# Long score products of heads 2 and 3 with 128 keys at once, between products with 64

## The chip, the cores and the metric

The kernel runs on one core of a Trainium2 chip. The metric is the device time of one execution in microseconds (us); a comparison is made on medians of several executions. The engines that matter here are TensorE (PE in the profile, with PEld for its weight loads), VectorE (DVE), ScalarE (ACT) and GpSimd (POOL). SyncE (SP) issues transfers.

## The reference

Thirty-two images of 256 channels and 32 x 32 = 1024 positions are normalized in 32 groups of channels, go through a causal attention of 8 heads with 32 channels each, and are added to the result. All is float32. Cut to the core:

```python
n = group_norm(x)                                   # 32 groups of 8 channels
q, k, v = q_w @ n + q_b, kv_w @ n + kv_b            # 256 channels each, 8 heads of 32
scores = einsum('bhqd,bhkd->bhqk', q, k) / sqrt(32)
attn = softmax(where(mask == 0, -10000, scores))    # mask: keys before the query alone
attn = where(mask == 0, 0, attn)
x = x + einsum('bhqk,bhkd->bhqd', attn, v)
```

## The kernel before

The 8 heads are two groups g of four, since four heads of 32 channels fill the 128 partitions: head j of a group lies in partitions 32j to 32j + 31 of the group's q and k. The 1024 queries are two halves of 512, and the keys are blocks of 128. Scores are made transposed, keys on partitions and queries along the free axis, so that their exponential can go straight into the product with v.

The work is cut into pieces (`piece`): a full piece is one key block against 512 queries (or, on the diagonal, one block against 384 queries and a second block against 128: two entries in `blocks`), a half piece one key block against 256 queries. A visit takes one full and one half piece of the four heads. Each group has 6 visits, an image 12, and the 32 images 384; in this document a visit and what is done beside it is called a round. In one third of the rounds the full piece has two blocks.

The loop over i runs through all rounds of all images. On TensorE a round has three stages: the scores of visit i (`scores`, matmuls in line 285), then a share of the projections of the next image (`product`, line 158: tiles pp and ppv), and then the values, the products of the exponentials of the visit before with v (`values`, line 373: tile acc). The order on TensorE, ScalarE, VectorE and GpSimd is the order in which the program names the work; no scheduler moves it.

Inside `scores`, three PSUM tiles of two banks each are taken: `pairs[0]` for the long products (the full piece) of heads 0 and 1, `pairs[1]` for those of heads 2 and 3, `pairs[2]` for the short products (the half piece) of all four, where head j and head j + 2 share a bank. A product contracts over the 32 channels of one head, so it occupies 32 rows of the array; its columns are the keys. `scores_of` makes it in pieces of `WIDE` = 64 keys, so a block of 128 keys takes two matmuls, with 64 columns of the array each. In the profile such a matmul has the shape 32*64 (rows * columns); the matmuls of projections and values are 128*32.

The order within the stage: short products of heads 2 and 3 (`first`), long products of heads 0 and 1 and then of 2 and 3 (for a piece of two blocks, the first block of all heads, then the second), and last the short products of heads 0 and 1. Before these last, TensorE waits on the semaphore `bank_free`, which the first short products raise, since the two share banks. The very last visit with a diagonal has an order of its own (the `else` branch). Then ScalarE takes three exponentials: of `pairs[0]`, `pairs[1]` (line 348) and `pairs[2]` (line 346), with 128 x 1024 elements each. GpSimd masks the diagonals (line 301), and VectorE adds up the exponentials for the softmax's denominators (line 381).

Of the kernel before, what the change touches and what calls it, by code (L numbers as in the profile page):

```python
# [17 lines left out]
P = 128  # L18
# [10 lines left out]
WIDE = 64  # L29
# [3 lines left out]
def tile_norm_attention_residual(  # L33
# [65 lines left out]
    def unshifted():  # L99
        live = {}  # L100
# [175 lines left out]
                blocks = [(k, slice(0, HALF), slice(0, HALF))]  # L276
            return g, hf, k, part, tuple(blocks)

        def scores_of(pc, pair, j, n=0):

            b, (g, hf, k, part, blocks) = pc
            rows = slice(HD * j, HD * (j + 1))
            kb, cols, of = blocks[n]
            return [
                nc.tensor.matmul(  # L285
                    pair[c : c + WIDE, cols], lhsT=live["k", b, g][rows, kb * P + c : kb * P + c + WIDE],
                    rhs=live["q", b, g][rows, hf * HALF + of.start : hf * HALF + of.stop],
                    start=True, stop=True, skip_group_check=True,
                )
                for c in range(0, P, WIDE)  # L290
            ]

        def mask(pc, e, heads=slice(0, 4)):


            g, hf, k, part, blocks = pc
            if k < hf * BPH:
                return
            n = len(blocks)
            diagonal = e[:, heads, : n * P].rearrange("p j (n q) -> p j n q", q=P)  # L300
            nc.gpsimd.affine_select(  # L301
                out=diagonal, in_=diagonal, pattern=[[0, heads.stop - heads.start], [0, n], [1, P]],
                compare_op=ALU.is_gt, fill=0.0, base=0, channel_multiplier=-1,
            )
            if k == 0:
                nc.gpsimd.memset(e[0:1, heads, 0:1], 1.0)

        def scores(b, full, half):


            tag = "e0" if full[2] == 0 else "e"
            name = f"{b}_{full[0]}_{full[1]}_{full[2]}"
            e = epool.tile([P, 4, HALF], F32, tag=tag, bufs=4 if tag == "e0" else 3, name=f"{tag}_{name}")
            eh = epool.tile([P, 4, HALFBANK], F32, tag="eh", bufs=4, name=f"eh_{name}")
            pairs = [ps_s.tile([P, 2, HALF], F32, tag="sT", name=f"sT_{name}_{a}") for a in range(3)]
            short = pairs[2].rearrange("p bank (n q) -> p bank n q", n=2)
            last = b == B - 1 and full[:2] == (NG - 1, NH - 1) and half[2] == NB - 2
            short_of = lambda heads, n: [m for j in heads for m in scores_of((b, half), short[:, j % 2, n, :], j)]
            long_of = lambda heads, n: [scores_of((b, full), pairs[j // 2][:, j % 2, :], j, n) for j in heads]


            if not last:
                first = short_of((2, 3), 1)
                for n in range(len(full[4])):
                    long_of(range(4), n)
            else:

                long_of(range(4), 0)
                long_of((0, 1), 1)
                first = short_of((2, 3), 1)  # L330
                long_of((2, 3), 1)

            for ins in first:
                ins.then_inc(bank_free, 1)
                tc.no_tile_sem_insts.add(ins.ins.name)
            live["free"] = live.get("free", 0) + len(first)
            wait = nc.tensor.wait_ge(bank_free, live["free"])
            for ins in first:
                tc.declare_no_dep(wait.ins, ins.ins, reason="the semaphore orders them")
            for j in range(2):  # L340
                for lo in scores_of((b, half), short[:, j, 0, :], j):
                    for ins in first:
                        tc.declare_no_dep(lo.ins, ins.ins, reason="the semaphore orders them")
            for a in range(3):
                if a == 2:
                    exp = nc.scalar.activation(eh.rearrange("p (n bank) q -> p bank n q", n=2), short, AF.Exp)  # L346
                else:
                    nc.scalar.activation(e[:, 2 * a : 2 * a + 2, :], pairs[a], AF.Exp)  # L348

            for ins in first:  # L350
                tc.add_to_no_dep_group(f"first_{name}", ins.ins)
                tc.add_to_no_dep_group("first", ins.ins)
            tc.declare_no_dep(exp.ins, group=f"first_{name}", reason="through the last two products")
            tc.declare_fence(exp.ins, group=f"first_{name}")
            for heads in (range(2), range(2, 4)) if last else (range(4),):
                mask(full, e, slice(heads.start, heads.stop))
            mask(half, eh)
            live["e", b, full], live["e", b, half] = e, eh
# [187 lines left out]
        with tc.manual_schedule(engines={ENG.PE, ENG.Activation, ENG.DVE, ENG.Pool}):  # L546
# [36 lines left out]
            for b in range(B):  # L583
                first, last = b * N, b == B - 1
# [30 lines left out]
            for i in range(B * N + 1):  # L615
                if i < B * N:
                    scores(i // N, *visits[i % N])
                for f in at.pop(i, ()):
                    f()
                pcs = products[(i - 1) % N] if i else ()  # L620
                if i == B * N:

                    sums(3, pcs, False)
                for pc in pcs:
                    values((i - 1) // N, pc, i <= (B - 1) * N or pc not in by_pe)
                if i == B * N - 2:

                    sums(3, [None, *pcs])
                if i == B * N - 1:
                    sums(3, pcs)  # L630
                for f in after.pop(i, ()):
                    f()
# [172 lines left out]
```

## Time and profile before

| | |
|---|---|
| median of 3 runs | 1822.24 us (1820.97 to 1822.68) |
| the profiled execution's own time | 1821.87 us |
| its span, first to last instruction | 1820.1 us |
| TensorE busy | 1807.9 us, 99% of the span |
| VectorE busy | 1655.6 us, 91% |
| ScalarE busy | 1480.0 us, 81% |
| GpSimd busy | 798.9 us, 44% |
| TensorE clock granted | 0.998 |

In a line of the profile, "L285 PE MATMUL sT<-q,k 32*64 32x256 f32 x14336 | 601.3, 447 | 0.2" would read: the matmuls of line 285 on TensorE write tile sT from q and k; the array shape is 32 rows by 64 columns, the moving operand has 32 partitions and 256 elements; there are 14336 of them; together they cover 601.3 us, one lasts 447 ns in the mean, and the engine was idle for 0.2 us before them. Matmuls overlap one another, so the mean of one times their number is far more than the time covered. The end of a matmul is modelled: what is sure is when it starts. A timeline line gives start and duration in us, and the number of instructions merged into it; the bracket at its end gives the idle time before, and what ended it.

### The profile page before, as it was taken

The page shows a single profiled execution, that of the slowest core. Times are in us where ns is not written, and L with a number is a line of the kernel's source. Part 1 is how long each engine was busy: PE and PEld are TensorE (multiplying, and loading weights), DVE is VectorE, ACT ScalarE, POOL GpSimd, SP SyncE. Part 2 cuts the span into 40 slices and gives each one's busy share as a digit, 9 for nine tenths or more (in the row PEclk, how much of TensorE's full clock was granted, in tenths as well). Part 3 has the DMA queues.
Part 4 walks back from the last instruction along what each step waited for, and adds up shares of the span by engine and source line. Part 5 has one row for each costly group of instructions (what it writes and reads, how often), then busy time and mean ns, then how long its engine had stood idle before and what let it go on. Part 6 is the DMA issues. An engine that isn't in the chain of part 4 may idle for free. (4 is left out here: it accounts for less than half of the span.)

```text
span 1820.1 us, 68098 instructions
## 1 busy us (share of the span) xinstructions
PE 1807.9 (99%) x30388; PEld 837.4 (46%) x30388; DVE 1655.6 (91%) x1762; ACT 1480.0 (81%) x1860; POOL 798.9 (44%) x774
## 2 busy tenths in 40 slices
PE   9999999999999999999999999999999999999997
PEld 5444444444444444444444444444444444444443
DVE  4799999999999999999999999999999999999988
ACT  6888878888888888788887888877888878888885
POOL 1444544535435445344354353443444544435532
PEclk9999999999999999999999999999999999999999
DMA  3457676676776766767767667676667676676662
GB/s 123 71 98 137 134 150 113 133 148 125 147 127 125 143 128 137 148 121 133 142 129 147 116 135 150 124 141 136 123 137 136 134 152 115 129 152 124 124 124 73
DMA packets 77836, 235.91 MB, mean 130 GB/s; under 512 B 20320, under 2 KB 21344, under 8 KB 61664
## 3 DMA queue, kind: packets, MB, share of 16 engines
q0 software_dynamic: 15872, 97.53, 40.1%
q1 hardware_dynamic: 61664, 133.96, 26.4%
q8 instruction: 239, 3.92, 0.9%
q14 instruction: 61, 0.50, 0.1%
HBM read 66.85 MB, written 34.57 MB: 56 GB/s over the span
## 5 line engine op out<-in xcount | busy, mean ns | idle before, releaser
L348 ACT ACTIVATE e<-sT 128x1024 f32<-128x1024 f32 x768 | 745.2, 1022 | 269.3 <-PE sT L285 214.5
L381 DVE TENSOR_TENSOR e<-e,e 128x1536 f32<-128x1536 f32 x376 | 632.5, 1682 | 17.7
L381 DVE TENSOR_TENSOR e<-e,eh 128x1024 f32<-128x1024 f32 x380 | 524.2, 1394 | 112.3 <-PE acc L373 92.8
L301 POOL TENSOR_SCALAR_AFFINE_SELECT e<-e 128x512 f32<-128x512 f32 (+1 forms) x257 | 381.9, 1486 | 549.6 <-ACT e L348 546.4
L285 PE MATMUL sT<-q,k 32*64 32x256 f32 (+3 forms) x14336 | 601.3, 447 | 0.2
L158 PE MATMUL pp<-xn,wT 128*32 128x512 f32 x4096 | 492.4, 598 | 0.1
L285 PEld LDWEIGHTS sT<-q,k 32*64 32x64 f32 x14336 | 353.3, 130 | 212.9 <-ACT eh L346 64.7
L373 PE MATMUL acc<-e,v 128*32 128x512 f32 (+2 forms) x4096 | 400.8, 486 | 0.0
L346 ACT ACTIVATE eh<-sT 128x1024 f32<-128x1024 f32 x384 | 395.6, 1030 | 0.0
L397 POOL DMA_DIRECT2D e<-e x248 | 202.0, 824 | 399.5 <-DMA e<-e 305.3
L158 PE MATMUL ppv<-wT,xn 128*32 128x256 f32 x4096 | 247.5, 382 | 0.0
L373 PEld LDWEIGHTS acc<-e,v 128*32 128x32 f32 x4096 | 133.1, 110 | 223.1 <-issue 192.1
L373 PE MATMUL acc<-eh,v 128*32 128x256 f32 x3072 | 224.6, 379 | 0.0
L158 PEld LDWEIGHTS pp<-xn,wT 128*32 128x32 f32 x4096 | 107.5, 109 | 237.2 <-issue 228.9
L373 PEld LDWEIGHTS acc<-eh,v 128*32 128x32 f32 x3072 | 98.8, 110 | 164.0 <-issue 153.0
L158 PEld LDWEIGHTS ppv<-wT,xn 128*32 128x32 f32 x4096 | 120.3, 109 | 110.8 <-issue 44.7
L301 POOL TENSOR_SCALAR_AFFINE_SELECT eh<-eh 128x512 f32<-128x512 f32 x128 | 166.7, 1302 | 0.6 <-ACT eh L346 0.2
L224 ACT ACTIVATE xn<-x,shift,rstd 128x512 f32<-128x512 f32 x124 | 103.1, 831 | 0.0
L484 DVE SCALAR_TENSOR_TENSOR rb<-rb,v_bias_col,x 128x512 f32<-128x512 f32 x124 | 94.0, 758 | 4.4
L238 ACT ACTIVATE k<-pp,qk_bias 128x512 f32<-128x512 f32 x128 | 89.8, 702 | 2.3 <-PE pp L158 1.2
L238 ACT ACTIVATE q<-pp,qk_bias 128x512 f32<-128x512 f32 x128 | 89.9, 702 | 1.0 <-PE pp L158 1.0
L410 DVE STREAM_TRANSPOSE turned<-folded 128x512 f32<-128x512 f32 x124 | 87.6, 706 | 2.2
(70 smaller groups left out, 665.8 us busy)
## 6 DMA issues: line engine op xcount, KB each, us to landing
e<-e POOLq DMA_DIRECT2D x124, 512.0 KB, 6.8
x<-in_x_dram SPq DMA_DIRECT2D x64, 512.0 KB, 6.3
e<-e POOLq DMA_DIRECT2D x124, 256.0 KB, 4.6
folded<-e SPq DMA_DIRECT2D x124, 256.0 KB, 3.9
rb<-inverses SPq DMA_DIRECT2D x124, 256.0 KB, 8.0
out_dram<-rb SPq DMA_DIRECT2D x124, 256.0 KB, 4.7
inverses<-inv_turned SPq DMA_DIRECT2D x31, 32.0 KB, 1.7
out_dram<-rb_last SPq DMA_DIRECT2D x3, 256.0 KB, 2.5
```

The source lines that it names most:

```text
L158: nc.tensor.matmul(out[part], lhsT=lhsT[:, part], rhs=rhs, start=start, stop=stop, skip_group_check=True)
L224: nc.scalar.activation(xn, xt, AF.Identity, bias=live["shift", b][:, g : g + 1], scale=rstd)
L238: nc.scalar.activation(live[key][:, cols], pp, AF.Identity, bias=qk_bias[:, n, g : g + 1], scale=(SCALE, 1.0)[n],)
L285: nc.tensor.matmul(pair[c : c + WIDE, cols], lhsT=live["k", b, g][rows, kb * P + c : kb * P + c + WIDE], rhs=live["q", b, g][rows, hf * HA ...
L301: nc.gpsimd.affine_select(out=diagonal, in_=diagonal, pattern=[[0, heads.stop - heads.start], [0, n], [1, P]], compare_op=ALU.is_gt, fill= ...
L346: exp = nc.scalar.activation(eh.rearrange("p (n bank) q -> p bank n q", n=2), short, AF.Exp)
L348: nc.scalar.activation(e[:, 2 * a : 2 * a + 2, :], pairs[a], AF.Exp)
L373: nc.tensor.matmul(acc[HD * j : HD * (j + 1), of], lhsT=live["v", b][:, kb, h * HD : (h + 1) * HD], rhs=e[:, j, cols], start=first, stop=l ...
L381: nc.vector.tensor_add(total[:, :, of], total[:, :, of], e[:, :, cols])
L397: nc.gpsimd.dma_start(out=total[:rows], in_=total[rows : 2 * rows], accum_op=ALU.add)
L410: nc.vector.transpose(turned, live["folded", b][:, j, :])
L484: nc.vector.scalar_tensor_tensor(rb, rb, v_bias_col[:, g : g + 1], xt[:, g, cols], ALU.add, ALU.add)
```

## The change

`scores_of` gets a parameter for the number of keys that a matmul takes, 128 unless it is told otherwise, and `short_of` and `long_of` hand it on. In every visit but the last, all products are still told 64, except the long ones of heads 2 and 3 (of the first block, where there are two), which come between the long products of heads 0 and 1 and what follows, and are now made as one matmul of 128 keys for each head, shape 32*128. In the last visit's own order the second blocks of all heads and the first short products take 128 keys. The short products that come last stay at 64.

```diff
-        def scores_of(pc, pair, j, n=0):
+        def scores_of(pc, pair, j, n=0, wide=P):
...
-                    pair[c : c + WIDE, cols], lhsT=live["k", b, g][rows, kb * P + c : kb * P + c + WIDE],
+                    pair[c : c + wide, cols], lhsT=live["k", b, g][rows, kb * P + c : kb * P + c + wide],
...
-                for c in range(0, P, WIDE)
+                for c in range(0, P, wide)
...
-            short_of = lambda heads, n: [m for j in heads for m in scores_of((b, half), short[:, j % 2, n, :], j)]
-            long_of = lambda heads, n: [scores_of((b, full), pairs[j // 2][:, j % 2, :], j, n) for j in heads]
+            short_of = lambda heads, n, wide=P: [
+                m for j in heads for m in scores_of((b, half), short[:, j % 2, n, :], j, 0, wide)
+            ]
+            long_of = lambda heads, n, wide=P: [
+                scores_of((b, full), pairs[j // 2][:, j % 2, :], j, n, wide) for j in heads
+            ]
...
-                first = short_of((2, 3), 1)
-                for n in range(len(full[4])):
-                    long_of(range(4), n)
+                first = short_of((2, 3), 1, WIDE)
+                long_of((0, 1), 0, WIDE)
+                long_of((2, 3), 0)
+                for n in range(1, len(full[4])):
+                    long_of(range(4), n, WIDE)
             else:
-                long_of(range(4), 0)
+                long_of(range(4), 0, WIDE)
                 long_of((0, 1), 1)
                 first = short_of((2, 3), 1)
                 long_of((2, 3), 1)
...
-                for lo in scores_of((b, half), short[:, j, 0, :], j):
+                for lo in scores_of((b, half), short[:, j, 0, :], j, 0, WIDE):
```

## The prediction

> **What bounds the kernel now.** I read the page first (shares, slices, costliest groups), then the groups kept apart by shape, then the timeline of one round in the middle of the run, then that round's matmuls in very narrow windows, and last the waits. The page's shares and groups:
>
> ```profile
> PE 1807.9 (99%) x30388; PEld 837.4 (46%) x30388; DVE 1655.6 (91%) x1762; ACT 1480.0 (81%) x1860; POOL 798.9 (44%) x774
> L285 PE MATMUL sT<-q,k 32*64 32x256 f32 (+3 forms) x14336 | 601.3, 447 | 0.2
> L346 ACT ACTIVATE eh<-sT 128x1024 f32<-128x1024 f32 x384 | 395.6, 1030 | 0.0
> ```
>
> PE is busy all the time and waits before L285 for 0.2 us in all; L346 counts 384 rounds (one short exponential each). So a microsecond added to PE in every round is a microsecond of the kernel. The timeline of a round (start, duration, engine, instructions; PE and PEld lines alone):
>
> ```profile
> 904.09 0.40 PE L373 MATMUL acc<-eh,v 128*32 128x256 f32 x4
> 904.42 0.64 PEld L285 LDWEIGHTS sT<-q,k 32*64 32x64 f32 x24 [0.41 <-issue]
> 904.42 1.55 PE L285 MATMUL sT<-q,k 32*64 32x256 f32 x32
> 905.25 0.27 PEld L285 LDWEIGHTS sT<-q,k 32*64 32x64 f32 x8 [0.19 <-PE sT L285]
> 905.90 0.16 PEld L158 LDWEIGHTS pp<-xn,wT 128*32 128x32 f32 x8 [0.38 <-issue]
> ...
> 906.35 0.13 PEld L158 LDWEIGHTS pp<-xn,wT 128*32 128x32 f32 x4 [0.30 <-issue]
> 906.78 0.13 PEld L158 LDWEIGHTS pp<-xn,wT 128*32 128x32 f32 x4 [0.30 <-issue]
> 907.21 0.13 PEld L373 LDWEIGHTS acc<-e,v 128*32 128x32 f32 x4 [0.30 <-issue]
> ```
>
> The score stage runs from 904.42 to 905.90: 1.48 us. It holds 16 products in the program but 32 matmuls on PE, so every float32 product makes two passes. In the projection after it, four column tiles (128*32) stream together and a new set of four starts every 0.43 us (906.35, 906.78, 907.21): 0.43 us is one pass over 512 columns, so 0.32, 0.215 and 0.107 for 384, 256 and 128. Now the arithmetic of the stage: heads 0 and 1 (array rows 0 to 63) have a long product (512) and a short one (256), 2 x 0.43 + 2 x 0.215 = 1.29 us; heads 2 and 3 (rows 64 to 127) have the same. The stage takes 1.48, not 2.58, so the two pairs of heads stream side by side, in different rows.
>
> Narrow windows in that stage (groups of matmuls by shape, their mean ns last but one column) show what a first pass pays:
>
> ```profile
> L285 PE MATMUL sT<-q,k 32*64 32x512 f32 x4 | 0.7, 638 | 0.0
> L285 PE MATMUL sT<-q,k 32*64 32x256 f32 x4 | 0.4, 425 | 0.0
> ...
> L285 PE MATMUL sT<-q,k 32*64 32x256 f32 x4 | 0.4, 374 | 0.0
> L285 PE MATMUL sT<-q,k 32*64 32x512 f32 x8 | 0.6, 587 | 0.0
> ```
>
> The first two lines are the passes just after the change from 128*32 to 32*64, the last two later passes: 51 ns longer each. The last values matmuls start at 904.11 and stream 0.215 us, to 904.33; the first load of the scores starts at 904.42. So **a change of tile shape costs 0.09 us in which nothing streams, and then an exposed weight load of 0.05 us**. Within one shape there is no such gap: the loads at 906.35 to 907.21 are pulled ahead under the matmuls that are streaming.
>
> **What the Trainium skill says.** "TensorEngine Tiling (Array Packing)", section Key Properties: changing the tiling mode, not just the tile, drains TensorE; its list of modes has 32x64 and 32x128 as two. The 0.09 us, the same from 128*32 to 32*64 and back (the stage's last matmuls start at 905.59, stream to 905.81, next load 905.90), agrees. But there all rows of the array change hands, so this trace doesn't show that rows which nobody else wants are drained too. "TensorE: Matmul & The Clock Gate", section LDWEIGHTS, prices a load at its columns / 1.2 ns: 27, 53 and 107 ns for 32, 64 and 128 columns. The trace's exposed part is 25 ns for 32 columns (617 against 592 ns in the projection) and 51 for 64: it agrees. Same page, section "What happens when you issue a matmul": weight loads are pulled ahead of running matmuls; the trace agrees within a shape.
>
> **The change, part by part.** In each of 383 rounds the long products of heads 2 and 3 (first block) go from four of 64 keys to two of 128: with two passes, 4 fewer matmuls and 4 fewer loads on PE, the same columns streamed (2 x 0.43 per row group, both halves of the keys already streamed side by side). The fewer instructions are worth nothing: they are issued 7 ns apart under streams of 430. No wait, DMA or instruction of another engine moves; the order of the queues is otherwise the same. What is added: PE passes short 2,3 and long 0,1 in shape 32*64, then long 2,3 in 32*128, then short 0,1 in 32*64: two more changes of shape inside a stage that had none. I take it that each drains the whole array. Times from the stage's start, one block (256 rounds):
>
> - long 0,1 starts its first pass at 0.03, second at 0.53 (0.43 + 0.05 exposed load + stagger), streams to 0.955. Short 2,3 has been done since 0.50, and its rows now stand idle.
> - drain 0.095: 1.05.
> - long 2,3 alone: exposed load of 128 columns, two passes: 0.107 + 2 x 0.43 + 0.007 stagger: 2.02. Rows 0 to 63 idle.
> - drain 0.095: 2.11. Short 0,1: 0.05 + 2 x 0.215 + 0.02: 2.61; then 0.09 to the next stage: 2.70.
>
> Against 1.48 that is **+1.22 us**. Check of the same bookkeeping on before: short 0,1 starts at 0.94 (when long 0,1 is done) and adds 0.43 + 0.02 + 0.09: 1.48. So 1.22 is the later start of short 0,1 (2.11 - 0.94 = 1.17) and its exposed load (0.05).
>
> Two blocks (127 rounds, 384 then 128 columns; 1.52 us now): long 0,1 to 0.74, drain to 0.835, long 2,3 0.107 + 2 x 0.32 + 0.01 to 1.59, drain to 1.69; then the 128-column blocks of all heads, 0.05 + 2 x 0.107 to 1.95, short 0,1 to 2.42, and 0.09: 2.51. **+1.0 us**.
>
> The last round has its own order (three products there also go to 128 keys): two changes of shape between stages that are otherwise parallel, 0.2 + 0.15 and some imbalance: +0.7 us at most.
>
> The unknown terms. The exposed 128-column load: the nearest row,
>
> ```profile
> L144 PEld LDWEIGHTS busy<-ident 128*128 128x128 f32 x6 | 0.7, 192 | 0.0
> ```
>
> lasts 192 ns, and loads of 32 and 64 columns (110 and 132 ns when hidden) expose 25 and 51, that is all but 81 to 85; 192 less 84 is 108, as the skill's price has it. Low end 55 (the transposes' first matmul, 327 ns against 272 later): -20 us over 384 rounds; high end the whole load, 192: +33. If the second pass's load were not pulled ahead either, another 0.11 to 0.19 a round, +41 to +74. A gain is excluded, as the load was hidden before. The drain: 0.06 to 0.11 a change, -27 to +12 us.
>
> What gives back: nothing on PE, which has no idle time to fill (0.2 us). What might wait anew: the next score stage needs the banks that ScalarE's exponentials free. Long 2,3 is done at 2.0 and short 0,1 at 2.6 of the stage, and exponentials of 1.0 us each end at about 4.3; a copy of k or q behind them (projection done at 2.70 + 1.74 = 4.44, copy 0.7 us) ends at about 5.3. The next stage starts at 4.62 + 1.22 = 5.84 (a round is 904.42 to 909.04 now). So nothing waits; ScalarE and VectorE keep their work (1480 and 1656 us) in a longer span and don't bound. That leaves 0.5 us of cover; a copy later than that would hold the next score stage up by the difference.
>
> Sum: 256 x 1.22 + 127 x 1.0 + 0.7 = 312 + 127 + 1 = +440. The profiled execution took 1821.9 us with a span of 1820.1; the median is 1822.2. Span after 2260; time **2262 us**.
>
> **The rivals.** *No drain where rows don't conflict* (not slower): PE may run 32*128 in rows 64 to 127 while 32*64 streams in rows 0 to 63. Then long 2,3 starts when short 2,3 is done, as now, and short 0,1 when long 0,1 is done; the stage ends at 1.48. For it: the tiles of the pairs share neither rows nor banks, and weight loads overlap across rows. Against: the 0.09 us in which no load is pulled ahead whenever the shape changes, and the skill's sentence. It decides if a change costs heads 2 and 3 under 0.03 us (their stream ends at 905.78, the stage's at 905.81): 1822 us, within 3 either way.
>
> *A change costs only the rows concerned*: rows 64 to 127 take drain and load twice, rows 0 to 63 run on. Long 2,3 then ends at 0.50 + 0.095 + 0.107 + 0.87 = 1.57 and the stage at 1.66: +0.18; with two blocks, a change more, +0.3. 256 x 0.18 + 127 x 0.3 = 84: 1906 us. For it: row groups have their own order of passes. Against: as above.
>
> That the change isn't what it says is excluded: the compiled order of PE has two 128-key products where four of 64 stood, and the other queues are identical.
>
> **How the numbers follow.** Whole drain 0.84, rows alone 0.07, none 0.09. The whole drain's terms give 2262 - 47 (both low ends) to 2262 + 57 (high load, high drain and a little of the second pass's load), so 2215 to 2320; that holds nearly all of its 0.84 and so 8 in 10 by itself. About 0.2% is what a measurement of this kernel tells from no change: of the last case 0.06 fall within it and 0.03 are faster.
>
> **What would show it.** L285's matmuls fall from 14336 to 12792 (383 x 4 + 12 fewer), 1544 of them 32*128. The one-block stage lasts 2.7 us, the two-block one 2.5. Inside it the loads of 32*128 start some 0.09 us after long 0,1 has streamed out; the first 32*128 pass is about 107 ns longer than the second. ScalarE's wait for L285 grows. If the loads of 32*128 instead start at about 0.5 us, while long 0,1 streams, the drain isn't there and I am wrong; if only the spacing of the stage's parts is off, a term of the sum is.

## The result and the profile after

The changed kernel takes 2250.62 us (four runs, 2250.35 to 2250.9) against 1821.61 us of the kernel before beside it: a ratio of 1.2356, 95% interval 1.2334 to 1.2377. Its profiled execution has a span of 2248.9 us, 428.8 more than the 1820.1 before.

The page of the changed kernel, shares and one cause of waiting:

```profile
PE 2236.9 (99%) x28844; PEld 796.7 (35%) x28844; DVE 1601.4 (71%) x1762; ACT 1540.7 (69%) x1860; POOL 771.6 (34%) x774
L354 ACT ACTIVATE e<-sT 128x1024 f32<-128x1024 f32 x768 | 770.6, 1023 | 435.2 <-PE sT L285 360.5
L285 PE MATMUL sT<-q,k 32*64 32x256 f32 x12792 | 1033.9, 448 | 0.0
```

PE has 1544 fewer matmuls and yet 429 us more of busy time; L285 covers 1033.9 us where it covered 601.3. (Its line in the page stands for all shapes, of which it names one.) The other engines have the same instructions in a longer span, and ScalarE's wait for the scores has grown from 214.5 to 360.5 us. The groups kept apart by shape show the new products; the first line is of the kernel before, the others of the changed one:

```profile
L285 PE MATMUL sT<-q,k 32*64 32x512 f32 x4096 | 382.0, 600 | 0.0
L285 PE MATMUL sT<-q,k 32*128 32x512 f32 x1024 | 288.6, 640 | 0.0
L285 PE MATMUL sT<-q,k 32*64 32x512 f32 x2048 | 278.3, 613 | 0.0
L285 PE MATMUL sT<-q,k 32*128 32x384 f32 x508 | 116.1, 533 | 0.0
L285 PE MATMUL sT<-q,k 32*64 32x384 f32 x1032 | 112.0, 507 | 0.0
```

Of the 512-query matmuls, 4096 covered 382.0 us before; now 3072 cover 288.6 + 278.3 = 566.9. One lasts 613 or 640 ns in the mean where it lasted 600, so the matmuls have hardly become slower: fewer of them run side by side.

The timeline of one score stage with one block, weight loads alone (start, duration, engine, instructions, idle time before):

```profile
1104.36 0.13 PEld L379 LDWEIGHTS acc<-eh,v 128*32 128x32 f32 x4 [0.30 <-issue]
1104.90 0.23 PEld L285 LDWEIGHTS sT<-q,k 32*64 32x64 f32 x16 [0.41 <-issue]
1105.94 0.30 PEld L285 LDWEIGHTS sT<-q,k 32*128 32x128 f32 x4 [0.81 <-ACT xn L224]
1107.00 0.21 PEld L285 LDWEIGHTS sT<-q,k 32*64 32x64 f32 x8 [0.76 <-issue]
1107.59 0.16 PEld L158 LDWEIGHTS pp<-xn,wT 128*32 128x32 f32 x8 [0.39 <-issue]
```

Before, 24 loads of the stage came in one group and the last 8 while matmuls were streaming. Now there are three groups, one for each stretch of one shape. The last second-pass matmul of long 0,1 starts at 1105.425 and streams 512 columns, 0.43 us, to 1105.85; the loads of the 32*128 products start at 1105.94, 0.09 us later. The short products of heads 2 and 3, in the rows that these loads want, had streamed out at about 1105.40: those rows stood idle for half a microsecond. The same 0.09 us stands before 1107.00, where the products of heads 0 and 1 in turn wait for the 32*128 ones. (The release that the bracket at 1105.94 names, a ScalarE instruction, is only the last semaphore update before: in all 384 rounds, at both changes of shape, the load stands the same 0.09 us behind the end of the stream, to within 4 ns.)

Two narrow windows in the same stage show the first 32*128 pass, and the second:

```profile
L285 PE MATMUL sT<-q,k 32*128 32x512 f32 x2 | 0.7, 692 | 0.0
...
L285 PE MATMUL sT<-q,k 32*128 32x512 f32 x2 | 0.6, 587 | 0.0
```

The first is 105 ns longer: the exposed load of 128 columns. The stage lasts 2.69 us (1104.90 to 1107.59). With two blocks, before (matmuls; the stage runs to the next line's start):

```profile
909.04 1.59 PE L285 MATMUL sT<-q,k 32*64 32x256 f32 x48
910.56 1.93 PE L158 MATMUL ppv<-wT,xn 128*32 128x256 f32 x32
```

and after (weight loads):

```profile
1122.42 0.23 PEld L285 LDWEIGHTS sT<-q,k 32*64 32x64 f32 x16 [0.41 <-ACT q L238]
1123.25 0.30 PEld L285 LDWEIGHTS sT<-q,k 32*128 32x128 f32 x4 [0.60 <-issue]
1124.10 0.42 PEld L285 LDWEIGHTS sT<-q,k 32*64 32x64 f32 x24 [0.55 <-issue]
1124.91 0.37 PEld L158 LDWEIGHTS ppv<-wT,xn 128*32 128x32 f32 x12 [0.38 <-issue]
```

The stage shown took 1.52 us before and takes 2.49 us now. Over all rounds the medians are 2.693 and 2.484 us, against 1.476 and 1.518 before: 256 x 1.217 + 127 x 0.966 = 311.6 + 122.7 = 434.3 us; the last round's stage goes from 2.09 to 2.29. The span has grown by 428.8, so some 6 us came back. Of these, 2.0 are four score stages of the kernel before that lasted up to 0.75 us longer than the others; the changed kernel has none. Another 2.7 are at the 31 places where a values stage is followed by a variance product (47.1 to 44.3 us up to the next stage).

### The profile page after: what moved, and what is told of

The parts are those of the page before. It is cut to its first block, busy times and chain, and to the rows that moved or that the text cites. A ratio compares the mean times of both kernels' runs of the same rounds, so it can differ in the third digit from the quotient of the medians.

```text
span 2248.9 us, 65010 instructions
## 1 busy us (share of the span) xinstructions
PE 2236.9 (99%) x28844; PEld 796.7 (35%) x28844; DVE 1601.4 (71%) x1762; ACT 1540.7 (69%) x1860; POOL 771.6 (34%) x774
## 4 chain that ended last, share of the span: by engine, by line
PE 99%; DVE 0%; DMA 0%; issue 0%; ACT 0%
PE sT L285 45%; PE acc L379 22%; PE pp L158 21%; PE ppv L158 11%; PE pd L424 0%; DMA x<-in_x_dram 0%; DVE st L168 0%; PE pv L158 0%; PE pm L158 0%; PE wt L137 0%; DVE rb_last L490 0%; DVE rb_last L480 0%; DVE turned L477 0%; PE busy L144 0%; DVE rb_last L489 0%
## 5 line engine op out<-in xcount | busy, mean ns | idle before, releaser
L354 ACT ACTIVATE e<-sT 128x1024 f32<-128x1024 f32 x768 | 770.6, 1023 | 435.2 <-PE sT L285 360.5
L285 PE MATMUL sT<-q,k 32*64 32x256 f32 x12792 | 1033.9, 448 | 0.0
L387 DVE TENSOR_TENSOR e<-e,eh 128x1024 f32<-128x1024 f32 x380 | 478.0, 1272 | 534.0 <-PE acc L379 419.0
L301 POOL TENSOR_SCALAR_AFFINE_SELECT e<-e 128x512 f32<-128x512 f32 (+1 forms) x257 | 357.1, 1389 | 990.6 <-ACT e L354 985.4
L387 DVE TENSOR_TENSOR e<-e,e 128x1536 f32<-128x1536 f32 x376 | 619.4, 1647 | 75.6 <-POOL e L301 64.3
L285 PEld LDWEIGHTS sT<-q,k 32*64 32x64 f32 x12792 | 311.4, 136 | 668.2 <-issue 453.1
L403 POOL DMA_DIRECT2D e<-e x248 | 201.5, 815 | 382.0 <-DMA e<-e 301.9
L254 ACT COPY v<-ppv 128x512 f32<-128x512 f32 x128 | 75.6, 590 | 53.1 <-PE ppv L158 53.1
L301 POOL TENSOR_SCALAR_AFFINE_SELECT eh<-eh 128x512 f32<-128x512 f32 x128 | 110.9, 866 | 0.5 <-ACT eh L352 0.3
L392 ACT COPY num<-acc 128x512 f32<-128x512 f32 x127 | 74.3, 585 | 48.8 <-PE acc L379 48.7
```

The source lines that it names most:

```text
L254: nc.scalar.copy(live["v", b][:, 2 * n : 2 * n + 2, :], pp)
L285: nc.tensor.matmul(pair[c : c + wide, cols], lhsT=live["k", b, g][rows, kb * P + c : kb * P + c + wide], rhs=live["q", b, g][rows, hf * HA ...
L301: nc.gpsimd.affine_select(out=diagonal, in_=diagonal, pattern=[[0, heads.stop - heads.start], [0, n], [1, P]], compare_op=ALU.is_gt, fill= ...
L387: nc.vector.tensor_add(total[:, :, of], total[:, :, of], e[:, :, cols])
L392: nc.scalar.copy(num, acc)
L403: nc.gpsimd.dma_start(out=total[:rows], in_=total[rows : 2 * rows], accum_op=ALU.add)
```

## The experiments

The trace after shows what happens; the experiments ask why. The theory is that each change of shape drains the whole array, so that the cost is rows that stand idle, with 0.09 us and an exposed load for each change. Its rivals: products of 128 keys are slow in themselves (A), each change has a fixed price whatever streams around it (B), a change is free and only overlap is lost (C). The granted clock was 0.997 to 0.999 in all profiles but the last experiment's (0.991).

**One shape for the whole stage, 128 keys.** The kernel before, with a width of 128.

```diff
-WIDE = 64
+WIDE = 128
```

> Every score product takes 128 keys, so the score stage has one shape, 32*128, from its start to its end. Theory (a change of shape drains the whole array; 128 keys cost nothing but a longer exposed load): the two pairs of heads stream side by side again. Only the stage's first load grows from 0.05 to 0.105 us exposed, less 0.01 of stagger: +0.04 us in each of 384 rounds, +15 us: 1837 us, one-block stage 1.52 us. Rival A (a product of 128 keys is slow in itself, or keeps the rows of other heads from streaming): the stage stays at or above the changed kernel's 2.69 us, 2250 us or more.

Measured 1825.33 us, ratio 1.0018 (1.0011 to 1.0026) to the kernel before. The stage's loads, from its timeline:

```profile
905.31 1.17 PEld L285 LDWEIGHTS sT<-q,k 32*128 32x128 f32 x16 [0.41 <-issue]
906.81 0.16 PEld L158 LDWEIGHTS pp<-xn,wT 128*32 128x32 f32 x8 [0.33 <-issue]
```

One group, 1.50 us. The two pairs of heads stream side by side in shape 32*128 as well, so rival A falls: products of 128 keys aren't slow in themselves. With eight or twelve of them in a round, where the changed kernel has two, they cost 3 us in place of 429. The theory's +15 us was too much: the exposed load is 0.054 us longer (105 against 51 ns), but with half as many matmuls ahead of long 0,1 and at the end, half of that is saved in stagger: the stage with one block goes from 1.476 to 1.503 us, and with two blocks it is even 0.005 shorter.

**The long products of all four heads with 128 keys, the short ones with 64.** The changed kernel, with this edit:

```diff
-                long_of((0, 1), 0, WIDE)
-                long_of((2, 3), 0)
+                long_of(range(4), 0)
```

(The last round keeps 64 keys throughout, here and in the next experiment.)

> Long products of all four heads (first block) take 128 keys, the rest 64: still two changes of shape inside the stage, as in the changed kernel, but the long products of both pairs of heads stream side by side. Theory (what costs is rows standing idle across a drain): short 2,3 to 0.50, drain to 0.59, longs to 1.575, drain to 1.665, short 0,1 and drain 0.59: 2.255 us, +0.78 with one block, +0.73 with two: 256 x 0.78 + 127 x 0.73 = 293: 2115 us. Rival B (each change of shape has a fixed price, 0.6 us, whatever streams): 2250 us as the changed kernel.

Measured 2109.54 us, ratio 1.158 (1.1561 to 1.1599). As many changes of shape as in the changed kernel, and 141 us less: a fixed price per change doesn't describe it. The loads of one stage:

```profile
1003.72 0.21 PEld L285 LDWEIGHTS sT<-q,k 32*64 32x64 f32 x8 [0.41 <-ACT q L238]
1004.31 0.31 PEld L285 LDWEIGHTS sT<-q,k 32*128 32x128 f32 x8 [0.39 <-issue]
1005.38 0.21 PEld L285 LDWEIGHTS sT<-q,k 32*64 32x64 f32 x8 [0.76 <-issue]
1005.97 0.16 PEld L158 LDWEIGHTS pp<-xn,wT 128*32 128x32 f32 x8 [0.39 <-issue]
```

The parts last 0.59, 1.07 and 0.59 us, as worked out (0.59, 1.075, 0.59). Here the two short pairs each have the array to themselves, which costs 0.43 us of streaming. In the changed kernel long 2,3 and short 0,1 have it to themselves, and long 0,1 for the half of its time in which short 2,3 is done: 0.86 us.

**Long 2,3 with 128 keys at the head of the stage.** The changed kernel, with these products moved:

```diff
-                first = short_of((2, 3), 1, WIDE)
-                long_of((0, 1), 0, WIDE)
                 long_of((2, 3), 0)
+                first = short_of((2, 3), 1, WIDE)
+                long_of((0, 1), 0, WIDE)
```

> The long products of heads 2 and 3 with 128 keys go to the head of the stage, all others follow with 64: one change of shape inside the stage in place of two. Theory (idle rows): 0.97 us for the long products alone, 0.09 drain, and then rows 0 to 63 need what the whole stage takes before: 1.06 + 1.48 = 2.54, +1.06; with two blocks 0.84 + 1.52 = 2.36, +0.84. 256 x 1.06 + 127 x 0.84 = 378: 2200 us. Rival B (fixed price of a change): half of the 429 us, 2036 us.

Measured 2192.64 us, ratio 1.2037 (1.2017 to 1.2057).

```profile
1003.57 0.30 PEld L285 LDWEIGHTS sT<-q,k 32*128 32x128 f32 x4 [0.41 <-ACT k L238]
1004.41 1.10 PEld L285 LDWEIGHTS sT<-q,k 32*64 32x64 f32 x40 [0.55 <-issue]
1005.89 0.16 PEld L158 LDWEIGHTS pp<-xn,wT 128*32 128x32 f32 x8 [0.38 <-issue]
```

One change of shape less, but only 58 us less than the changed kernel, where a fixed price would have given back 214. (The stage shown has two blocks: 0.84 us for the long products alone, then 1.48 for the rest.) Rows 0 to 63 still wait for the whole of long 2,3. Rival B falls with both runs.

**The bare price of a change.** The kernel before, with one product of 128 keys and 2 queries ahead of each stage; it writes into a tile that the real product overwrites.

```diff
             if not last:
...
+                nc.tensor.matmul(
+                    pairs[1][:, 0, 0:2], lhsT=live["k", b, g][rows, kb * P : (kb + 1) * P],
+                    rhs=live["q", b, g][rows, hf * HALF : hf * HALF + 2],
+                    start=True, stop=True, skip_group_check=True,
+                )
                 first = short_of((2, 3), 1)
```

> The kernel before with one more product of 128 keys and 2 queries at the head of each score stage but the last (its result is overwritten by the real product): one change of shape more in each round, with next to nothing streamed in it. This is the bare price of a change where nothing else is running. Theory: exposed 128-column load 0.105, two tiny passes about 0.03, drain 0.09: 0.23 us x 383 = 88: 1910 us. Rival B (fixed price 0.6 us): 2050 us. Rival C (all of the loss is lost overlap, a change itself is free): within 10 us of 1822.

Measured 1940.19 us, ratio 1.0649 (1.0631 to 1.0666): 118 us, 0.308 us a round, where 0.23 was expected. Rivals B and C both miss: a change is not free, and not 0.6 us. The loads of one stage:

```profile
962.86 0.29 PEld L326 LDWEIGHTS sT<-q,k 32*128 32x128 f32 x2 [0.41 <-issue]
963.17 0.64 PEld L285 LDWEIGHTS sT<-q,k 32*64 32x64 f32 x24
```

The missing 0.08 us: the second pass of the tiny product starts 0.132 us into the stage and streams 2 columns, so by the 0.09 us rule the next shape could load at 0.22. But its weight load, 184 ns, began at 0.106 and ends at 0.290; the next load starts at 0.306. So it looks as if the next shape waits for loads in flight too; in the real kernel a load ends long before its stream, and this doesn't show.

**32 keys.** Would narrower products expose less and be faster? The kernel before, with a width of 32.

```diff
-WIDE = 64
+WIDE = 32
```

> Every score product takes 32 keys: one shape, 32*32, in the stage, twice as many matmuls and loads. Theory (the first load's exposed part goes by its columns, and matmuls are issued 7 ns apart): exposed load 0.025 in place of 0.05, but eight matmuls in place of four ahead of the first long product (+0.027) and eight at the stage's end (+0.027): +0.03 us a round, +11 us: 1833 us. Rival (the narrower the products, the less is exposed, issue is free): -0.026 us a round, 1812 us, faster than before.

Measured 2064.28 us, ratio 1.1319 (1.1303 to 1.1334): both expectations missed. The exposed load is right (first passes of 256 columns last 399 ns, against 374 later: 25 ns). But the stage lasts 1.90 us, and 2.45 with two blocks:

```profile
1024.82 1.36 PEld L285 LDWEIGHTS sT<-q,k 32*32 32x32 f32 x64 [0.41 <-ACT xn L224]
1026.72 0.16 PEld L158 LDWEIGHTS pp<-xn,wT 128*32 128x32 f32 x8 [0.54 <-issue]
```

The first 16 products (short 2,3 and long 0,1) start 7 ns apart; of long 2,3 only one starts at 0.46 us, the other seven from 0.68 us on, 42 ns apart; most of the short 0,1 that follow are 17 ns apart. A stage with one block of the kernel before has just 16 such products (of 64 keys, two matmuls each).

**More than 16 products, in the old shape.** The kernel before, with sixteen tiny products of 64 keys (each head, both halves of the keys, twice) ahead of the stage.

```diff
             if not last:
...
+                for c in range(0, 2 * P, WIDE):
+                    for j in range(4):
...
+                        nc.tensor.matmul(
+                            pairs[j // 2][at : at + WIDE, j % 2, 0:2],
...
                 first = short_of((2, 3), 1)
```

> The kernel before with 16 more products of 64 keys and 2 queries at the head of each score stage but the last (their results are overwritten by the real products): 32 products in the stage, as where all take 32 keys, but in the shape 32*64 and with next to nothing streamed. It asks why products of 32 keys cost 0.42 us a round. Theory D (only so many products are ready when the stage begins, and later ones come 0.04 us apart): the real loads after the first 16 or so products start some 0.04 us apart and the stage takes about 2.0 us, 2020 us in all. Theory E (the shape 32*32 is itself slow to issue): the loads go on 7 ns apart, bound by the tiny products' own loads (16 products x 2 passes over 8 tiles x 0.053 = 0.21 us): stage 1.7 us, 1910 us.

Measured 2041.03 us (two runs), ratio 1.1211 (1.1178 to 1.1243). The stage takes 1.83 us, between the two forecasts:

```profile
1008.86 0.35 PEld L329 LDWEIGHTS sT<-q,k 32*64 32x64 f32 x32 [0.41 <-issue]
1009.10 1.21 PEld L285 LDWEIGHTS sT<-q,k 32*64 32x64 f32 x32
1010.69 0.16 PEld L158 LDWEIGHTS pp<-xn,wT 128*32 128x32 f32 x8 [0.39 <-issue]
```

After the sixteen, new products start 17 ns apart, neither 7 nor 42. The stages' regular lengthening makes 256 x 0.358 + 127 x 0.328 = 133 of the 220 us; most of the rest is in some 40 stages, most of them score stages, that last 1 to 5 us longer, spread over the whole span. So the sixteen added products cost 0.33 to 0.36 us a stage in this shape as well, more than the 0.21 us worked out from their own loads. But the number alone isn't shown to decide: the kernel before has 24 products in its stages with two blocks, and of these only the last four have their loads 17 ns apart. How the 42 ns come about with 32 keys, and what ends the long stalls, these runs don't settle. It doesn't touch the change, which lowers the number of products.

## Why the prediction was right

The forecast was 2262 us, 11 above the measured 2251, with the likeliest case as its mechanism. By its steps:

- *PE bounds every round, so each added microsecond counts.* Right: 434 us were added to the score stages and 429 came out.
- *A change of shape drains the whole array*, rows that nobody else wants included. The prediction took this from a sentence of the Trainium skill ("TensorEngine Tiling (Array Packing)", Key Properties: a change of the tiling mode drains TensorE) and from changes in which all rows changed hands, and said that the trace before didn't show it. The trace after does: the 32*128 loads stand at 1.04 us of the stage, behind long 0,1, and not at 0.5. The rival without a drain (1822 us) and the one with a drain of the rows concerned (1906) are out. That the shape is what matters, and not the 128 keys, is shown by the run with 128 keys throughout: 1825 us.
- *The drain*, 0.095 taken, 0.09 measured at both changes.
- *The exposed 128-column load*, 0.107 taken between ends of 0.055 and 0.192: 0.105. The Trainium skill's price ("TensorE: Matmul & The Clock Gate", LDWEIGHTS: columns / 1.2 ns, so 107) fits this exposed part; the whole record of such a load lasts 181 ns. The way from the durations of loads came to 108 partly by luck: it took 192 ns less 84 hidden, and the runs show 181 less 76.
- *The second pass's load is pulled ahead*: yes. The second 32*128 pass starts 0.533 us after the first, which is 0.43 of stream and the first pass's 0.105; nothing of the second's load shows.
- *One block +1.22*: 1.217. Marks within the stage were forecast at 1.05, 2.11 and 2.70 us, measured at 1.04, 2.10 and 2.69.
- *Two blocks +1.0*: 0.966. Marks 0.835, 1.69 and 2.51 against 0.83, 1.68 and 2.48; the term was 0.034 too high, which makes 4 us of the 11.
- *The last round*, 0.7 at most: 0.2. (Six products there go to 128 keys, in three pairs of heads, where the text has three.)
- *Nothing gives back*: 6 us did, which the prediction didn't have, and which make most of the rest of the 11. The term was taken to be nothing because PE showed no idle time. But the ends of matmuls are modelled: a matmul of 512 columns is shown as 587 ns, 0.16 us longer than it streams, and a late start can lie under that. The four longer score stages were in the trace before, and the 0.2 us of idle time ahead of L285 didn't show them.
- *No new wait on ScalarE*: right. In the round shown, the exponentials end at 1109.06, 4.2 us after the stage's start (4.3 forecast), the k copy at 1110.27 (5.4), and the next stage starts at 1110.31 without being late: the values stage before it has 16 matmuls and its usual length. Over the whole run the 317 values stages directly ahead of a score stage take 552.8 us, and took 553.0 before. The cover in that round was thin; the 0.5 us in the text were worked out for a longer round.

## What to carry to other kernels

Within a run of matmuls that overlap in different rows of the array, keep one shape: here one odd shape in the middle cost 1.2 us a round, of which only 0.3 were drains and loads, and 0.9 the rows that stood idle while the odd products had the array alone. To price such a change before it is made, write the stage as one timeline for each group of rows, put a barrier across all of them at each change of shape (0.09 us and the exposed load), and see how long each group of rows waits. Between 64 and 128 keys the width itself hardly matters: one or the other throughout differs by 0.2%. That isn't so for 32 keys, which cost 13%.

## What the runs showed of the hardware

- In a change of shape the next shape's weight load starts 0.09 us after the last column has streamed (128*32 to 32*64, 32*64 to 32*128, and back), in rows that had been idle for half a microsecond too, and then exposes 25, 51 and 105 ns for 32, 64 and 128 columns. It seems to wait for loads in flight as well (bare change, 0.308 us and not 0.23).
- Not expected: in stages of 32 products, the later ones start 17 ns apart (64 keys), or 42 and 17 ns (32 keys), in place of 7, and 32 keys throughout cost 241 us although they expose the shortest load. Why is open.
